# The values' bias of a graph attention moved behind the division, and the values scaled tile by tile

## The chip, the core and the metric

The kernel runs on one core of one Trainium2 chip. A core has a matrix engine (TensorE, PE in the profile), a vector engine (VectorE, DVE), an engine for activation functions (ScalarE, ACT), a general engine (GpSimd, POOL) and an engine that issues transfers (SyncE, SP). [...] The metric is the time of one execution on the device in microseconds (us).

## The reference, cut to what matters

Two layers work on 32 graphs ("batches" below) of 512 nodes with 256 features. Each layer has a graph part and a feed-forward part. The change touches the graph part of the second layer, an attention with 4 heads of 64 features:

```python
h = jnp.einsum('bnd,hde->bhne', nodes_embed, W)
e_src = jnp.einsum('bhne,hte->bhtn', h, a_src)
e_dst = jnp.einsum('bhne,hte->bhtn', h, a_dst)
...
weight = jax.nn.leaky_relu(weight, negative_slope=0.01)
weight = jnp.where(node_adj[:, None] == 0, NEG, weight)
attention = jax.nn.softmax(weight, axis=-1)
dst = jnp.einsum('bhij,bhje->bhie', attention, h) + bias[None, :, None, :]
out = jax.nn.relu(dst) + h
mu = out.mean(axis=-1, keepdims=True)
var = out.var(axis=-1, keepdims=True)
out = (out - mu) / jnp.sqrt(var + EPS) * ln_gamma + ln_beta
```

The weights of a node sum to one. So a bias added to every value `h` before the weighted mean comes out of the mean unchanged; it may be added to the values or to the mean.

## The kernel before, in words

`layer1_plain` computes the second layer. It is written as Python generators that are woven into each other step by step, and a scheduler then orders the instructions of each engine from what was emitted. `attentions` weaves the attention of batch b (`attention(b)`) with the preparation of batch b + 1 (`prepare(b + 1)`) by the counts `TURNS - 4` and `STEPS`; `mixer` runs the feed-forward part for a group of `GB` = 2 batches and pulls the attentions along at a rate `PACE`, in which `STEPS` stands too. So the layer repeats in pairs of batches: the scan of a group (`xp`, `zp`, `yp`, `yTp`, `oTp`, `vp`), then the products `outp` of its two batches, then the slice weights `sw` of the next two, which are softmaxes: `lgp` on TensorE, an exponential on ScalarE (L1336), a product, a sum, a reciprocal and a second product on VectorE (L1337 to L1342), and then the products `yTp` (L1347).

`prepare(b)` gathers the rows of `x` by four indirect DMAs on GpSimd's queue (L1154; five buffers of `x`, so a gather waits for the store of an older batch), normalises them (L1126 to L1133), adds `beta` on GpSimd (L1167), transposes them and computes, for each of NT = 4 tiles of 128 nodes, `hp`: the values of the four heads and the two scores. ScalarE makes four things of each tile (L1183 to L1186): `mine`, the factor exp(s) in the last column of `hv`, `other`, and `ht`, the plain values. Then one instruction on GpSimd adds the bias to all four tiles, from `ht` into `hv` (L1189), and a step of the generator ends. Behind it `mine` is transposed on TensorE (`minep`, L1193), copied by ScalarE, written to DRAM (L1197) and read back spread over all partitions as `own`, by four DMAs on SyncE's queue (L1200). At last VectorE multiplies each tile of the values by its factor (L1202).

`attention(b)` makes the weights on VectorE, one instruction for each head and tile, from `own` and the mask (L1213), and accumulates values and denominators on TensorE (`avp`, `adp`). It takes them back by transposes (`dp`, `bp`), and VectorE divides them into `av`, two heads at a time (L1275). `norm(b, av)` goes on in steps woven into the next batch's attention: the relu and the sum with `ht` (L1290), the mean, the centring, ScalarE's squares, the variance, GpSimd's power (L1300), and the sum into `x` (L1304). GpSimd also adds the output bias to `x` (L1328).

Of the kernel before, what the change touches and what calls it, by code (L numbers as in the profile page):

```python
# [19 lines left out]
P = 128  # L20
N = 512
D = 256
NT = N // P
# [74 lines left out]
def layer0_sorted(tc, ident, eps, x, adj, w, x2s, ranks, over, following):  # L98
# [13 lines left out]
    CAPS = [24, 9, 7, 6, 5, 5, 5] + 5 * [4] + 4 * [3] + 7 * [2] + 9 * [1]  # L112
    STEPS = [16, 12, 9, 8, 7, 6, 5, 4, 3, 2, 1, 0]
    NC = len(STEPS)
    LEAD = 16
# [12 lines left out]
    with ExitStack() as ctx:  # L128
# [22 lines left out]
        steps = cst.tile([P, NC], F32, tag="steps", name="steps")  # L151
        for i, n in enumerate(STEPS):
            nc.gpsimd.memset(steps[:, i : i + 1], n + 0.5)
# [711 lines left out]
def layer1_plain(tc, ident, eps, x2s, ranks, adj, w, out, over, ps):  # L865
# [3 lines left out]
    nc = tc.nc  # L869
# [3 lines left out]
    AH, _, HO = w["W"].shape  # L873
# [13 lines left out]
    HE = HO + 1  # L887
    AP = AH // 2
    TURNS = AP * NT + 6
    STEPS = 15  # L890
    WANTED = 68
    AHEAD = 3
    ATT = 2 * (AHEAD + 2) + AP + 1
# [1 line left out]
    AHEAD_X = 2 * GB + 1  # L895
    PACE = 1.04 * GB * (TURNS + STEPS) / WANTED

# [3 lines left out]
    with ExitStack() as ctx:  # L901
# [6 lines left out]
        def const(name, shape, src):  # L908
            t = ctile(name, shape)
            nc.sync.dma_start(t, src)  # L910
            return t

        def psum(tag, name):
            return ps.tile([P, N], F32, tag=tag, name=name)
# [29 lines left out]
        abias = const("abias", [P, AH * HO], w["gnn_bias"].rearrange("h e -> (h e)").partition_broadcast(P))  # L944
# [203 lines left out]
        def prepare(b):  # L1148

            while b >= AHEAD_X and b - AHEAD_X not in stored:  # L1150
                yield True
            xt = xs[b] = sb.tile([P, NT, D], F32, tag="x", name=f"x{b}", bufs=AHEAD_X)
            for t in range(NT):
                nc.gpsimd.indirect_dma_start(  # L1154
                    out=xt[:, t, :], out_offset=None, in_=x2s[b // SEG],
                    in_offset=bass.IndirectOffsetOnAxis(
                        ap=ranks[:, b * NT + t : b * NT + t + 1].bitcast(U32), axis=0))

            hv = sb.tile([P, NT, AH, HE], F32, tag="hv", name=f"hv{b}")
            xn = hv.rearrange("p t h e -> p (t h e)")[:, : NT * D].rearrange("p (t d) -> p t d", t=NT)  # L1160
            edged = masks(b) if b not in masked else range(3)
            for i, _ in enumerate(edged):
                if i < 3 or b not in masked:
                    yield
                if i == 2:
                    normed(xt, xn, f"c{b}")
                    nc.gpsimd.tensor_add(xt, xt, beta.unsqueeze(1).to_broadcast([P, NT, D]))  # L1167
                    yield
            mask = masked.pop(b)
            xnT = yield from turned(xn, "x3T", f"x3T{b}")  # L1170
            yield


            ht = sb.tile([P, NT, AH * HO], F32, tag="ht", name=f"ht{b}")
            other = sb.tile([P, NT, AH], F32, tag="other", name=f"other{b}")
            mine = sb.tile([P, AH, NT], F32, tag="mine", name=f"mine{b}")
            for t in range(NT):
                ph = psum("any", f"hp{b}_{t}")
                for c in range(DC):
                    nc.tensor.matmul(ph[:, : AH * (HO + 2)], xnT[:, c, t * P : (t + 1) * P], wa[:, c, :],  # L1180
                                     start=c == 0, stop=c == DC - 1)
                d = ph[:, AH * HO : AH * HO + AH]
                nc.scalar.activation(mine[:, :, t], ph[:, AH * (HO + 1) : AH * (HO + 2)], AF.Exp, scale=1.0 - SLOPE)  # L1183
                nc.scalar.activation(hv[:, t, :, HO], d, AF.Exp)
                nc.scalar.activation(other[:, t, :], d, AF.Exp, scale=SLOPE - 1.0)
                nc.scalar.copy(ht[:, t, :], ph[:, : AH * HO])  # L1186
                yield

            nc.gpsimd.tensor_add(hv[:, :, :, :HO], ht.rearrange("p t (h e) -> p t h e", h=AH),  # L1189
                                 abias.rearrange("p (h e) -> p h e", h=AH).unsqueeze(1).to_broadcast([P, NT, AH, HO]))  # L1190
            yield
            pt = psum("any", f"minep{b}")
            nc.tensor.transpose(pt[: AH * NT, :P], mine.rearrange("p h t -> p (h t)"), ident)  # L1193
            row = sb.tile([AH * NT, P], F32, tag="turned", name=f"turned{b}", bufs=1)
            nc.scalar.copy(row, pt[: AH * NT, :P])
            own_row = dr.tile([AH, N], F32, tag="own", name=f"ownd{b}")
            nc.sync.dma_start(own_row.rearrange("h (t p) -> (h t) p", p=P), row)  # L1197
            own = [wide("own", f"own{b}_{h}", AH + 1) for h in range(AH)]
            for h in range(AH):
                nc.sync.dma_start(own[h], own_row[h].partition_broadcast(P))  # L1200
            for t in range(NT):
                nc.vector.tensor_mul(hv[:, t, :, :HO], hv[:, t, :, :HO], hv[:, t, :, HO:].to_broadcast([P, AH, HO]))  # L1202
            ready[b] = mask, ht, hv, other, own
            yield

# [10 lines left out]
        def attention(b):  # L1216

            mask, ht, hv, other, own = ready[b]
            xt = xs[b]
            av = sb.tile([P, NT, AH, HO], F32, tag="av", name=f"av{b}", bufs=1)  # L1220
            turns = [(q, j) for j in range(NT) for q in range(AP)]

            def begin(b, n):
                q, j = turns[n]
                if (b, 2 * q, j) not in weighed:
                    weigh(b, q, j)

            def back(src, kind):

                dst = psum("pv", f"{kind}{b}")  # L1230
                for t in range(NT):
                    nc.tensor.transpose(dst[:, t * P : (t + 1) * P], src[:, t * P : (t + 1) * P], ident)
                return dst

            for n in range(AHEAD):
                begin(b, n)
            pv = [psum("pv", f"avp{b}_{q}") for q in range(AP)]
            for i, (q, j) in enumerate(turns):
                if i + AHEAD < len(turns):
                    begin(b, i + AHEAD)  # L1240
                elif b + 1 in ready:
                    begin(b + 1, i + AHEAD - len(turns))

                if q + 1 == AP:
                    ends = dict(start=j == 0, stop=j == NT - 1)
                    for p in range(AP):
                        for k in range(2 * HO // HW):
                            h, e = 2 * p + k * HW // HO, k * HW % HO
                            nc.tensor.matmul(pv[p][k * HW : (k + 1) * HW, :], hv[:, j, h, e : e + HW],  # L1249
                                             weighed[b, h, j], **ends)  # L1250
                    if j == 0:
                        pd = psum("pv", f"adp{b}")
                    for h in range(AH):
                        nc.tensor.matmul(pd[h * HW : (h + 1) * HW, :], hv[:, j, h, HO:].to_broadcast([P, HW]),
                                         weighed.pop((b, h, j)), **ends)
                yield
                if unfinished and i != 2:
                    next(unfinished[0], None)
                    yield
                    if i > 2:  # L1260
                        unfinished.pop()
            dT = wide("att", f"adT{b}", ATT)
            nc.scalar.copy(dT, pd)
            vT = [wide("att", f"avT{b}_{q}", ATT) for q in range(AP)]
            for q in range(AP):
                nc.scalar.copy(vT[q], pv[q])
            yield
            dt = back(dT, "dp")
            rs = sb.tile([P, NT, AH], F32, tag="rs", name=f"rs{b}")
            nc.vector.tensor_scalar_max(rs, dt.rearrange("p (t h e) -> p t h e", t=NT, h=AH)[:, :, :, 0], 1e-30)  # L1270
            nc.vector.reciprocal(rs, rs)
            for q in range(AP):
                bt = back(vT[q], f"bp{q}_")
                heads = slice(2 * q, 2 * q + 2)
                nc.vector.tensor_mul(av[:, :, heads, :], bt.rearrange("p (t h e) -> p t h e", t=NT, h=2),  # L1275
                                     rs[:, :, heads].unsqueeze(3).to_broadcast([P, NT, 2, HO]))
                yield
            unfinished.append(norm(b, av))

# [28 lines left out]
        def attentions():  # L1308
            yield from prepare(0)
            for b in range(B):  # L1310
                nxt = prepare(b + 1) if b + 1 < B else iter(())
                yield from woven(attention(b), TURNS - 4, nxt, STEPS)
            for _ in unfinished[0]:
# [926 lines left out]
```

## Time and profile before

| what | us |
|---|---|
| median of 3 runs | 4453.05 |
| lowest and highest | 4452.75, 4458.42 |
| the profiled execution's own time | 4459.08 |
| its span | 4456.4 |
| busy: TensorE, VectorE, ScalarE, GpSimd | 3922.0, 3347.2, 2291.6, 1718.8 |

The profile is of one execution. Its span goes from the first instruction to the last, and its own time is 2.7 us longer. Lines such as L1202 are lines of the kernel before; a row of a group gives the engine, the operation, what is written and read, the shape and how often. A row of a tile gives the least, median and largest duration in ns. In the timeline the first two columns are the start and the duration in us, and a bracket at the end of a row tells how long the engine stood idle ahead of it and who ended that.

### The profile page before, as it was taken

The page shows a single profiled execution, that of the slowest core. Times are in us where ns is not written, and L with a number is a line of the kernel's source. Part 1 is how long each engine was busy: PE and PEld are TensorE (multiplying, and loading weights), DVE is VectorE, ACT ScalarE, POOL GpSimd, SP SyncE. Part 2 cuts the span into 40 slices and gives each one's busy share as a digit, 9 for nine tenths or more (in the row PEclk, how much of TensorE's full clock was granted, in tenths as well). Part 3 has the DMA queues.
Part 4 walks back from the last instruction along what each step waited for, and adds up shares of the span by engine and source line. Part 5 has one row for each costly group of instructions (what it writes and reads, how often), then busy time and mean ns, then how long its engine had stood idle before and what let it go on. Part 6 is the DMA issues. An engine that isn't in the chain of part 4 may idle for free.

```text
span 4456.4 us, 57911 instructions
## 1 busy us (share of the span) xinstructions
PE 3922.0 (88%) x20311; PEld 2470.6 (55%) x20311; DVE 3347.2 (75%) x7008; ACT 2291.6 (51%) x4756; POOL 1718.8 (39%) x2036
## 2 busy tenths in 40 slices
PE   5568898899988999888997899999999999999987
PEld 4454565566656656545554455555555555555555
DVE  6668887897788987877766777767677877778763
ACT  3345565566564665556654544544545444454433
POOL 2357644664446644454314232332222232332220
PEclk8679999999999999989998999999999999999998
DMA  5546543664436543564422111111111111111100
GB/s 133 160 144 223 190 130 122 210 200 139 156 117 213 187 147 129 162 201 167 138 81 67 36 53 57 56 48 58 51 43 42 53 55 55 58 48 58 41 15 16
DMA packets 235107, 474.21 MB, mean 106 GB/s; under 512 B 38299, under 2 KB 114075, under 8 KB 234804
## 3 DMA queue, kind: packets, MB, share of 16 engines
q0 software_dynamic: 98688, 315.94, 22.2%
q1 hardware_dynamic: 136116, 154.46, 11.0%
q8 instruction: 162, 2.65, 0.2%
q14 instruction: 141, 1.16, 0.1%
HBM read 413.16 MB, written 57.16 MB: 106 GB/s over the span
## 4 chain that ended last, share of the span: by engine, by line
DVE 34%; PE 32%; DMA 11%; issue 9%; POOL 9%; ACT 5%; SPq 0%; POOLq 0%; DVEq 0%; ACTq 0%
DVE att L1213 5%; DVE acc L637 4%; PE clsp L623 3%; PE avp L1249 3%; PE po L652 3%; PE gatep L623 3%; DMA rows<-table,xs 2%; PE yTp L1347 2%; DVE sw L1337 2%; DVE sw L1342 2%; DVE best L598 2%; DMA rows<-table,tops 2%; DVE sst L1340 2%; DMA best<-table,xs 2%; PE xp L1400 1%
## 5 line engine op out<-in xcount | busy, mean ns | idle before, releaser
L623 PE MATMUL clsp<-xnT,wc 128*128 128x512 f32 x1024 | 520.8, 627 | 49.7 <-ACT cls L625 37.6
L623 PE MATMUL gatep<-xnT,wg 128*128 128x512 f32 x1024 | 499.8, 607 | 10.5 <-ACT gate L625 7.7
L652 PE MATMUL po<-wd,acc 128*128 128x256 f32 x2048 | 455.4, 381 | 6.1 <-DVE acc L641 3.8
L1213 DVE SCALAR_TENSOR_TENSOR att<-own,other,mask 128x512 f32<-128x512 f32 x512 | 392.9, 796 | 79.0 <-DMA own<-ownd 79.0
L652 PEld LDWEIGHTS po<-wd,acc 128*128 128x128 f32 x2048 | 388.3, 191 | 72.1 <-issue 9.2
L598 DVE SCALAR_TENSOR_TENSOR best<-rows,xs,best 128x1024 f32<-128x1024 f32 x212 | 274.4, 1295 | 121.9 <-ACT best L592 76.4
L637 DVE SCALAR_TENSOR_TENSOR acc<-past,fld,acc 128x512 f32<-128x512 f32 x448 | 345.7, 775 | 24.9 <-ACT past L636 16.9
L632 ACT ACTIVATE acc<-tz,fld 128x512 f32<-128x512 f32 x256 | 198.8, 777 | 269.3 <-PE tz L630 240.1
L623 PEld LDWEIGHTS gatep<-xnT,wg 128*128 128x128 f32 x1024 | 196.0, 196 | 252.3 <-issue 197.9
L636 ACT ACTIVATE past<-tz,fld 128x512 f32<-128x512 f32 x448 | 291.4, 693 | 68.1 <-DVE acc L637 66.6
L1347 PE MATMUL yTp<-sw,x 128*128 128x512 f32 x512 | 264.6, 655 | 64.3 <-DVE sw L1342 59.6
L595 POOL DMA_INDIRECT rows<-table,xs x212 | 249.5, 1177 | 171.6 <-DVE best L598 119.0
L1249 PE MATMUL avp<-att,hv 128*32 128x512 f32 x2048 | 298.9, 607 | 5.6 <-DVE att L1213 5.6
L623 PEld LDWEIGHTS clsp<-xnT,wc 128*128 128x128 f32 x1024 | 181.5, 198 | 188.1 <-issue 111.8
L434 PE MATMUL pm<-h,adj 128*128 128x258 f32 (+1 forms) x1024 | 181.2, 324 | 99.9 <-DVE keep L427 33.7
L1300 POOL TENSOR_TENSOR mu<-mu,eps 128x16 f32<-128x16 f32 x32 | 111.6, 3487 | 391.1 <-DVE mu L1299 391.0
L1335 PE MATMUL lgp<-wsl,x4T 128*128 128x512 f32 x512 | 242.8, 613 | 15.7 <-ACT sw L1336 6.8
L1154 POOL DMA_INDIRECT x<-x2s,ranks x128 | 135.9, 1062 | 298.1 <-DVE att L1213 148.1
L625 ACT ACTIVATE gate<-gatep,fld 128x512 f32<-128x512 f32 x256 | 175.5, 685 | 142.6 <-PE gatep L623 123.8
L553 POOL DMA_INDIRECT xs<-rows_of,order x128 | 156.1, 1219 | 221.5 <-DVE acc L637 100.8
L1567 PE MATMUL outp<-v,swT 128*128 128x256 f32 x1024 | 227.6, 381 | 0.0
L625 ACT ACTIVATE cls<-clsp,fld 128x512 f32<-128x512 f32 x256 | 176.1, 688 | 93.9 <-PE clsp L623 55.6
(599 smaller groups left out, 8978.1 us busy)
## 6 DMA issues: line engine op xcount, KB each, us to landing
adj<-in_adj POOLq DMA_DIRECT2D x128, 256.0 KB
ai<-in_adj SPq DMA_DIRECT2D x128, 256.0 KB
own<-ownd SPq DMA_DIRECT2D x128, 256.0 KB
rows_of<-keep SPq DMA_DIRECT2D x32, 550.0 KB
x<-in_x SPq DMA_DIRECT2D x32, 512.0 KB
x2s<-xs SPq DMA_DIRECT2D x32, 512.0 KB
out<-x SPq DMA_DIRECT2D x32, 512.0 KB
rows<-table,xs POOLq DMA_INDIRECT x212
```

The costliest lines, as they stand in the source:

```text
L595: nc.gpsimd.indirect_dma_start(out=row, out_offset=None, in_=table, in_offset=bass.IndirectOffsetOnAxis(ap=idxs[:, k : k + 1].bitcast(U32) ...
L598: nc.vector.scalar_tensor_tensor(m, row, vals[:, k : k + 1], m, ALU.add, ALU.max)
L623: nc.tensor.matmul(pf, wf[:, c, f * P : (f + 1) * P], xnT[:, c, :], start=c == 0, stop=c == DC - 1)
L625: nc.scalar.activation(o, pf, fn, bias=fld[:, f, bf : bf + 1], scale=1.0 if fn == AF.Gelu else 0.5)
L636: nc.scalar.activation(r, z, AF.Relu, bias=fld[:, f, AT + b : AT + b + 1])
L637: nc.vector.scalar_tensor_tensor(y, r, fld[:, f, CH + b : CH + b + 1], y, ALU.mult, ALU.add)
L652: nc.tensor.matmul(po[:, i, :], acc[f][:, t * P : (t + 1) * P], wd[:, f, :], start=f == 0, stop=f == FC - 1)
L1213: nc.vector.scalar_tensor_tensor(e, own[h], other[:, j, h : h + 1], mask[:, j, :], ALU.max, ALU.mult)
L1249: nc.tensor.matmul(pv[p][k * HW : (k + 1) * HW, :], hv[:, j, h, e : e + HW], weighed[b, h, j], **ends)
L1335: nc.tensor.matmul(pf, xnT[:, c, t * P : (t + 1) * P], wsl[:, c, :], start=c == 0, stop=c == DC - 1)
L1347: nc.tensor.matmul(py, xn[:, t, c * P : (c + 1) * P], sw[:, t, :], start=t == 0, stop=t == NT - 1)
L1567: nc.tensor.matmul(po[:, :D], swT[:, k, t * P : (t + 1) * P], v[:, k, :], start=k == 0, stop=k == KC - 1)
```

## The change

The bias is no longer added to the values. The division's result `av` gets it instead, for two heads at a time, by GpSimd. The values are scaled from `ht` straight into `hv`, by VectorE: tile t - 1 right after ScalarE's four instructions on tile t, and the last tile after the loop. The step that ended behind the old addition is gone, so `STEPS` is 14 instead of 15.

```diff
-    STEPS = 15
+    STEPS = 14
...
+            def values(t):
+                nc.vector.tensor_mul(hv[:, t, :, :HO], ht[:, t, :].rearrange("p (h e) -> p h e", h=AH),
+                                     hv[:, t, :, HO:].to_broadcast([P, AH, HO]))
+
             for t in range(NT):
...
                 nc.scalar.copy(ht[:, t, :], ph[:, : AH * HO])
+                if t:
+                    values(t - 1)
                 yield
 
-            nc.gpsimd.tensor_add(hv[:, :, :, :HO], ht.rearrange("p t (h e) -> p t h e", h=AH),
-                                 abias.rearrange("p (h e) -> p h e", h=AH).unsqueeze(1).to_broadcast([P, NT, AH, HO]))
-            yield
+            values(NT - 1)
             pt = psum("any", f"minep{b}")
...
-            for t in range(NT):
-                nc.vector.tensor_mul(hv[:, t, :, :HO], hv[:, t, :, :HO], hv[:, t, :, HO:].to_broadcast([P, AH, HO]))
             ready[b] = mask, ht, hv, other, own
...
                 nc.vector.tensor_mul(av[:, :, heads, :], bt.rearrange("p (t h e) -> p t h e", t=NT, h=2),
                                      rs[:, :, heads].unsqueeze(3).to_broadcast([P, NT, 2, HO]))
+
+                nc.gpsimd.tensor_add(av[:, :, heads, :], av[:, :, heads, :],
+                                     abias.rearrange("p (h e) -> p h e", h=AH)[:, heads, :].unsqueeze(1)
+                                     .to_broadcast([P, NT, 2, HO]))
                 yield
```

## The prediction, made before the changed kernel was run

> **What bounds the kernel now.** The change touches the second layer alone, from 2400 us to the end. I read the page first (the whole span, and the chain that ended last), then the table by stages for the steady part of that layer, then the groups of TensorE there, then the two tiles that the change handles, and last the timeline of one pair of batches.
>
> ```profile
> span 4456.4 us, 57911 instructions
> PE 3922.0 (88%) x20311; PEld 2470.6 (55%) x20311; DVE 3347.2 (75%) x7008; ACT 2291.6 (51%) x4756; POOL 1718.8 (39%) x2036
> ...
> DVE 34%; PE 32%; DMA 11%; issue 9%; POOL 9%; ACT 5%; SPq 0%; POOLq 0%; DVEq 0%; ACTq 0%
> ```
>
> ```profile
> sum 1600.00, PE 1486.21 PEld 887.36 DVE 1183.05 ACT 790.15 POOL 468.84; mean PE 185.78 PEld 110.92 DVE 147.88 ACT 98.77 POOL 58.61
> ```
>
> The second fence is the sum row of the stages from 2600 to 4200 us. TensorE (PE) is busy 1486.2 of 1600 us, 92.9%. So at most 7.1% of this part can be won without giving TensorE less work. The layer goes in pairs of batches; in the chain of waits the first products of the scan (`xp`) start at 3036.44 and at 3162.74, so a pair takes 126 us and TensorE is idle for some 8.9 us of it. Who holds it up stands in the groups of the stretch 2600 to 4250:
>
> ```profile
> L1347 PE MATMUL yTp<-sw,x 128*128 128x512 f32 x432 | 227.5, 665 | 61.3 <-DVE sw L1342 56.8 <-DVE sst L1341 2.7 <-ACT ai L1094 0.6
> L1335 PE MATMUL lgp<-wsl,x4T 128*128 128x512 f32 x428 | 201.5, 607 | 11.2 <-ACT sw L1336 6.8 <-DVE x L1569 2.9 <-DVE mask L1085 1.1
> L1535 PE MATMUL oTp<-yT,hoT 128*128 128x128 f32 x416 | 49.9, 278 | 12.4 <-ACT yT L1529 12.4
> ```
>
> The largest part, 59.5 us, is the product of the slice weights waiting for VectorE (DVE) to finish their softmax. So VectorE sets the end only where it is late with `sw`. Adding the idle stretches in the timeline of PE over eleven pairs gives 3.9 us a pair in the half of the even batch, 2.9 us in that of the odd one (1.9 before `yTp`, 1.0 before `rnp`), and 1.0 before `oTp`.
>
> VectorE's own two long waits here (tiles `hv` and `att`, the first with its row for GpSimd):
>
> ```profile
> L1202 DVE TENSOR_TENSOR hv<-hv x128: 415/419/427, 2409.2 to 4260.7; 128x256 f32<-128x256 f32 x128
> L1189 POOL TENSOR_TENSOR hv<-ht,abias x32: 2327/2355/7253, 2404.6 to 4256.7; 128x1024 f32<-128x1024 f32 x32
> ...
>   POOL hv L1189: 177.5, 31
> ...
>   DMA own<-ownd: 79.0, 15
> ```
>
> 177.5 us in 31 waits is 5.7 us a batch, but only some of that reaches TensorE: most falls where TensorE has other work queued.
>
> [...] (VectorE and GpSimd rows of the timeline):
>
> ```profile
> 2890.28 2.92 POOL L1167 TENSOR_TENSOR x<-x,beta 128x1024 f32<-128x1024 f32 x1 [10.31 <-ACT hv L1133]
> 2891.00 2.75 DVE L1213 SCALAR_TENSOR_TENSOR att<-own,other,mask 128x512 f32<-128x512 f32 x1
> ...
> 2411.74 10.68 DVE L1213 SCALAR_TENSOR_TENSOR att<-own,other,mask 128x512 f32<-128x512 f32 x16
> 2417.41 7.25 POOL L1189 TENSOR_TENSOR hv<-ht,abias 128x1024 f32<-128x1024 f32 x1 [10.47 <-ACT ht L1186]
> ```
>
> A weight of 0.74 us took 2.75 beside an addition; an addition of 2.35 took 7.25 behind a row of sixteen weights. The old addition nearly always ran while VectorE stood waiting for it, so it cost no lock; the new ones run among the weights. [...] here 2.355 us against 1.217 for 128x1024. No row has GpSimd's addition of 128x512. Bounds: half of 2.355 is 1.18, and no size makes it dearer than 2.36. I take 1.25 us each.
>
> **Part 1, the old addition goes (32 of 2.355 us), and the scaling follows each tile.** In the odd batch of the pair at 3200 us, VectorE waits from 3250.9 to 3259.80 and scales until 3261.8, one piece of it inside the softmax. ScalarE's last copy of `ht` ends at 3257.34. With the new code three tiles are scaled before that and the fourth ends at about 3257.9. The next work, the softmax of `sw`, needs ScalarE's exponential, which ends at 3259.09; it started at 3260.82. So 1.6 us earlier, and 0.34 us of scaling has left the chain: 2.0 us. Against 1.9 us of TensorE's idle time before `yTp` I take 1.3 us, since not each pair has it in this place. In the even batch (wait 3317.2 to 3321.36) nothing is won by this: VectorE then waits for `msp` until 3323.66 and for `own` until 3328.74.
>
> **Part 2, one step less in the preparation moves the transpose of `mine`.** The instruction order of the two built programs shows it: in the even batches from 2 to 30 `minep` stands ahead of `oTp` and `msp` in 1 of 15 before and in 12 of 15 after, so it moves in 11. In the pair at 3300 us the last exponential of `mine` ends at 3318.51, but `minep` ran at 3323.54, and the chain ownd, own, att followed until 3328.74. Placed right after `yTp` (ends 3318.33), its copy waits for ScalarE's copy of `yT` (ends 3319.39) and is done near 3319.6 instead of 3324.10. The two DMAs keep their 4.6 us, and SyncE's queue is clear (the last `ai` load ahead was issued at 3316.24): `att` starts at 3324.2, 4.5 us earlier. By 11/15 that is 3.3 us of lead for VectorE. TensorE has its `vp` and `outp` products until some 3342, so nothing shows at once; it shows where `sw` is late afterwards. The order also puts `bp1` of the odd batch ahead of the second `outp` group in 12 of 14 pairs (4 before), so that its division comes before those sums.
>
> **Part 3, the new additions: 64 of 1.25 us.** Each waits for its division on VectorE (L1275, 0.68 us[...]), and the norm's first instruction (L1290) waits for both. Even batches: divisions end at 0 and 0.6; the first addition runs 0.2 to 1.45, beside the second division. Then come five weights (3.3 us) and the norm; the first weight stands until 1.45 (0.85 lost). The second addition either wins the lock (1.25 lost) or starves until the weights end and the norm waits 1.4: 2.1 us lost either way. Odd batches: the order leaves one sum and one weight (1.0 us) between division and norm, and the norm comes at 3.4 instead of 1.6: 1.8 us lost. At least 0.9 us (the adds find gaps), at most 2.6 us (both in full). Behind the additions in GpSimd's queue stand `mu`'s power and, in odd batches, the eight gathers of `x`; those waited for the store of an older `x` anyway (start 3338.98), and I cost them at nothing as long as `bp1` comes first.
>
> **The sum per pair.** Odd half: `yTp` gains 1.3; the lead of 2.0 us is eaten by the lock (2.1) before `rnp`, whose 1.0 stays. Even half: lead 3.3 - 1.8 = 1.5 us off the 3.9. `oTp`: `minep` fills 0.3 of its 1.0. Total 3.1 us, over 15 pairs 47 us. The profiled execution took 4459.1 us (the span and 2.7 around it), 6.0 more than the median of 4453.05; 4459.1 - 47 - 6 gives 4406.
>
> **Rivals.**
> 1. *The lock cancels the gain.* With 2.6 us lost in each half, leads of 2.0 and 3.3 leave nothing in the odd half and 0.7 us in the even; new waits of `minep`'s neighbours eat that. For it: VectorE's atts are in rows, as at 2411.74. Against: VectorE is busy only 74% here (1183 of 1600). Time 4453.
> 2. *Slower: the gathers queue behind the additions.* Where `bp1` still comes after the second `outp` (3342.35 in this trace), the division ends near 3344 and the additions near 3346.7, so the gathers start 7.7 us late; VectorE's statistics of the next `x` (L1126) wait for them in order, with the softmax behind. The leads of 1.5 and the gains of 1.6 elsewhere cover 3.1 us of delay; from there it decides. For it: L1126 already waits 43.0 us on these DMAs. Against: the order of `bp1`. At 5 us a pair, 1.9 x 15 = 28 us: 4481.
> 3. *More than forecast.* If VectorE is never late with `sw`, 6 of 8.9 us go: 90 us, 4363. For it: the chain holds GpSimd's addition and both `own` DMAs in every pair. Against: the lock, and TensorE's clock at 0.97 to 0.99 already.
>
> **How the numbers follow.** Chances: forecast 0.57, rival 1 0.15, rival 2 0.21, rival 3 0.07. The forecast alone spans 4385 to 4432, from the bounds of the lock (0.9 to 2.6 us) and of what TensorE gets of each lead. With the other cases the range is 4375 to 4475. What the measurement can tell from no change is 0.2%, 9 us: faster is under 4444. That gives 0.64 faster (forecast, rival 3, a little of rival 1), 0.13 the same, 0.23 slower.
>
> **What would show it.** Right: VectorE's wait on `hv` falls from 177.5 us to below 90 and ends at ScalarE's copy; the wait for `own` (79.0) falls by half or more; `yTp`'s wait for `sw` (56.8 in the stretch) falls to about 30; TensorE's share rises from 92.9% to about 95%; single atts of about 2 us stand beside the new additions. Wrong: L1126's wait for the gathers grows well over 43 us, or the norm's first instruction waits over 2 us a batch for GpSimd.

## The result and the profile after

| | before | after |
|---|---|---|
| median, us | 4452.9 (4 runs, 4450.26 to 4458.42) | 4553.83 (4 runs, 4550.85 to 4562.9) |
| ratio after to before | | 1.0228, 95% interval 1.0211 to 1.0246 |
| profiled execution: span, own time | 4456.4, 4459.08 | 4552.2, 4553.97 |
| mean period of a pair of batches, us | 123.5 | 129.9 |

The change makes the kernel 2.3% slower, 101 us, where 47 us of gain were forecast. The period is the mean distance between the first scan products `xp` of two groups, over 14 pairs; 14 times 6.4 us is 90 us, so nearly all of the loss is in the steady part of the second layer.

From the page of the kernel after: the span, the busy times, and the shares of the chain that ended last.

```profile
span 4552.2 us, 57959 instructions
...
PE 3950.6 (87%) x20311; PEld 2480.8 (54%) x20311; DVE 3432.5 (75%) x7008; ACT 2291.2 (50%) x4756; POOL 1737.8 (38%) x2068
...
PE 37%; DVE 31%; DMA 9%; POOL 9%; issue 8%; ACT 5%; SPq 0%; POOLq 0%; DVEq 0%; ACTq 0%
```

VectorE (DVE) is busy 85 us longer with the same 7008 instructions. The table by stages of the kernel after, 2600 to 4200 us as in the prediction: its last stage and the sum. A stage's row has its length, the busy time and number of instructions of PE, PEld, DVE, ACT and POOL, the granted TensorE clock, the DMA share and GB/s.

```profile
4000.00:4200.00 200.00, 174.36 (x1083) 107.64 (x1082) 139.41 (x268) 89.12 (x236) 63.67 (x46) 0.91 0.19 57
sum 1600.00, PE 1431.04 PEld 849.30 DVE 1186.73 ACT 743.51 POOL 470.60; mean PE 178.88 PEld 106.16 DVE 148.34 ACT 92.94 POOL 58.83
```

TensorE (PE) was busy 92.9% of this stretch and is now 89.4%. Of a pair that is 8.8 us of idle time before (7.1% of 123.5) and 13.7 after (10.6% of 129.9): 4.9 of the 6.4 us are gaps. The other 1.5 us are longer work, and the clock fits that: the granted clock averages 0.958 over the eight stages, 0.978 before, and is down to 0.91 in the last. The clock record of both traces holds two rates only, full and half, and a pair has 11.5 us at half rate, 5.9 before. In these pairs each stretch at half rate comes behind 3.413 us in which TensorE was idle for 45% of the time or more (the last section has the numbers). So more gaps came here with a lower clock, and a pair grew by more than its gaps.

Which gaps? The groups of TensorE in the stretch 2600 to 4250, after:

```profile
L1354 PE MATMUL yTp<-sw,x 128*128 128x512 f32 x416 | 211.6, 650 | 64.8 <-DVE sw L1349 56.2 <-DVE mask L1085 8.0
L1342 PE MATMUL lgp<-wsl,x4T 128*128 128x512 f32 x406 | 205.9, 643 | 20.6 <-ACT sw L1343 8.1 <-DVE stc L1126 4.5 <-DVE mask L1085 3.4
...
L1542 PE MATMUL oTp<-yT,hoT 128*128 128x128 f32 x384 | 46.1, 278 | 8.0 <-ACT yT L1536 7.4 <-ACT turned L1200 0.6
...
L1084 PE MATMUL maskp<-identb,a 128*128 128x128 bf16 x396 | 38.7, 230 | 38.5 <-DVE mask L1085 32.7 <-ACT sw L1343 4.3 <-DVE x L1576 1.6
```

The wait for `sw` before `yTp` is what it was (56.2 us after 56.8), in 26 batches instead of 27. New is a product that the prediction does not name: `maskp`, which transposes the adjacency, waits 32.7 us for VectorE's cast of an earlier mask (3.3 before). The waits of the same stretch (engine and line, what it waited for, us in total, times, longest), first of the kernel before:

```profile
DVE att L1213 <- DMA own<-ownd: 72.8, 13, 7.3
...
DVE stc L1126 <- DMA x<-x2s,ranks: 31.6, 35, 1.7
...
DVE av L1303 <- POOL mu L1300: 19.8, 13, 2.1
...
PE maskp L1084 <- DVE mask L1085: 3.3, 4, 1.0
```

and of the kernel after:

```profile
DVE hv L1179 <- ACT ht L1191: 83.3, 55, 3.1
...
DVE av L1310 <- POOL mu L1307: 70.5, 22, 6.4
...
DVE stc L1126 <- DMA x<-x2s,ranks: 32.7, 22, 3.5
...
DVE att L1216 <- DMA own<-ownd: 28.9, 20, 5.4
...
DVE av L1297 <- POOL av L1281: 12.5, 12, 1.2
```

VectorE's waits moved much as forecast. The wait on `hv` now ends at ScalarE's copy, though over the whole run it fell only from 177.5 to 104.9 us and not below 90. The wait for `own` has fallen by more than half, the gathers cost no more in total, and the norm's first instruction (L1297) hardly waits for the additions. TensorE's two signs failed: neither did `yTp` wait less, nor did its busy share rise. The wait that grew is the second of the kernel after: the norm's last product (L1303 before, L1310 now) waits for GpSimd's power of the variance, 70.5 us against 19.8, at most 6.4 us at a time against 2.1. One such place in the timeline of the kernel after, first VectorE, then GpSimd, then TensorE:

```profile
2995.19 0.17 DVE L1306 TENSOR_SCALAR mu<-mu 128x16 f32<-128x16 f32 x1
2995.27 0.75 DVE L1216 SCALAR_TENSOR_TENSOR att<-own,other,mask 128x512 f32<-128x512 f32 x1
3000.54 1.23 DVE L1310 TENSOR_TENSOR av<-av,mu 128x1024 f32<-128x1024 f32 x1 [4.52 <-POOL mu L1307]
3001.68 0.68 DVE L1085 CAST mask<-maskp 128x512 uint8<-128x512 bf16 x1
...
3003.41 3.84 DVE L1344 TENSOR_TENSOR sw<-sw,ebsl 128x512 f32<-128x512 f32 x2
...
2995.27 1.02 POOL L1154 DMA_INDIRECT x<-x2s,ranks  x1 [0.19 <-issue]
2996.60 0.95 POOL L1154 DMA_INDIRECT x<-x2s,ranks  x1 [0.30 <-issue]
2997.57 2.93 POOL L1307 TENSOR_TENSOR mu<-mu,eps 128x16 f32<-128x16 f32 x1
...
3002.41 0.59 PE L1084 MATMUL maskp<-identb,a 128*128 128x128 bf16 x4 [8.98 <-DVE mask L1085]
```

The variance is ready at 2995.36. GpSimd has two gathers to issue first, and its power of only 16 numbers in each partition takes 2.93 us. VectorE stands 4.52 us, and the mask's cast and the softmax of `sw`, which come behind the product in its order, start at 3001.68 and 3003.41; TensorE, which needs the cast, stands 8.98 us. In the kernel before the softmax stood ahead of that product in each of these odd batches, and gave the power time. The softmax of batch b - 1 has eight products on VectorE, four with `ebsl` (L1337) and four with `sst` (L1342). How many of them stand ahead of the norm's last product of the odd batch b in VectorE's order, for b = 3 to 29:

```text
before, e2, e4               8 in 14 of 14
after, e1, e3, e8, e9        8 in 3, 0 in 11 of 14
e6, e10                      0 in 14 of 14
e11                          0 or 1 in 9, 7 or 8 in 5 of 14
e5, e7, e13, e15             8 in 14 of 14
e12, e14                     7 or 8 in 14 of 14
```

### The profile page after: what moved, and what is told of

The parts are those of the page before. It is cut to its first block, busy times and chain, and to the rows that moved or that the text cites. A ratio compares the mean times of both kernels' runs of the same rounds, so it can differ in the third digit from the quotient of the medians.

```text
span 4552.2 us, 57959 instructions
## 1 busy us (share of the span) xinstructions
PE 3950.6 (87%) x20311; PEld 2480.8 (54%) x20311; DVE 3432.5 (75%) x7008; ACT 2291.2 (50%) x4756; POOL 1737.8 (38%) x2068
## 4 chain that ended last, share of the span: by engine, by line
PE 37%; DVE 31%; DMA 9%; POOL 9%; issue 8%; ACT 5%; SPq 0%; POOLq 0%; DVEq 0%; ACTq 0%
DVE att L1216 5%; PE avp L1252 4%; DVE acc L637 4%; PE clsp L623 3%; PE gatep L623 3%; PE po L652 3%; PE yTp L1354 2%; DMA rows<-table,xs 2%; DVE best L598 2%; DVE sw L1344 2%; PE hp L1185 2%; PE adp L1257 2%; POOL x L1154 2%; PE lgp L1342 2%; DMA rows<-table,tops 2%
## 5 line engine op out<-in xcount | busy, mean ns | idle before, releaser
L623 PE MATMUL clsp<-xnT,wc 128*128 128x512 f32 x1024 | 521.6, 628 | 56.8 <-ACT cls L625 43.9
L1216 DVE SCALAR_TENSOR_TENSOR att<-own,other,mask 128x512 f32<-128x512 f32 x512 | 405.4, 821 | 32.5 <-DMA own<-ownd 32.3
L1354 PE MATMUL yTp<-sw,x 128*128 128x512 f32 x512 | 256.3, 643 | 67.7 <-DVE sw L1349 56.2
L1252 PE MATMUL avp<-att,hv 128*32 128x512 f32 x2048 | 308.8, 613 | 6.3 <-DVE att L1216 6.1
L1342 PE MATMUL lgp<-wsl,x4T 128*128 128x512 f32 x512 | 258.6, 643 | 25.2 <-ACT sw L1343 9.7
L434 PEld LDWEIGHTS pm<-h,adj 128*128 128x128 f32 x1024 | 149.7, 210 | 127.9 <-issue 71.0
L1574 PEld LDWEIGHTS outp<-v,swT 128*128 128x128 f32 x1024 | 192.2, 190 | 30.3 <-ACT v L1566 5.4
```

The source lines that it names most:

```text
L434: nc.tensor.matmul(pm[:, : c1 - c0], a[:, i, t * P : (t + 1) * P], h[:, i, c0:c1], start=i + c0 == 0, stop=i + 1 == NT and c0 > 0)
L623: nc.tensor.matmul(pf, wf[:, c, f * P : (f + 1) * P], xnT[:, c, :], start=c == 0, stop=c == DC - 1)
L1216: nc.vector.scalar_tensor_tensor(e, own[h], other[:, j, h : h + 1], mask[:, j, :], ALU.max, ALU.mult)
L1342: nc.tensor.matmul(pf, xnT[:, c, t * P : (t + 1) * P], wsl[:, c, :], start=c == 0, stop=c == DC - 1)
L1354: nc.tensor.matmul(py, xn[:, t, c * P : (c + 1) * P], sw[:, t, :], start=t == 0, stop=t == NT - 1)
L1574: nc.tensor.matmul(po[:, :D], swT[:, k, t * P : (t + 1) * P], v[:, k, :], start=k == 0, stop=k == KC - 1)
```

## The experiments

The runs came in four groups; the kernel before, run along with them, had medians of 4459.2, 4465.39, 4459.17 and 4460.44 us. So kernels are compared by their ratios to it.

| run | what | median | ratio, 95% interval |
|---|---|---|---|
| e1 | after, no additions | 4492.71 | 1.0080, 1.0060 to 1.0101 |
| e2 | before, bias moved only | 4474.38 | 1.0034, 1.0025 to 1.0043 |
| e3 | before, step dropped only | 4520.04 | 1.0151, 1.0126 to 1.0177 |
| e4 | after, step put back | 4481.78 | 1.0059, 1.0038 to 1.0080 |
| e5 | after, pace 1.00 | 4525.0 | 1.0129, 1.0112 to 1.0146 |
| e6 | before, pace 1.06 | 4514.63 | 1.0101, 1.0080 to 1.0121 |
| e7 | e3, pace 1.00 | 4517.1 | 1.0115, 1.0094 to 1.0137 |
| e8 | e3, product doesn't wait for the power | 4455.71 | 0.9978, 0.9965 to 0.9990 |
| e9 | after, product doesn't wait for the power | 4484.67 | 1.0054, 1.0037 to 1.0070 |
| e10 | e3, product two turns later | 4571.34 | 1.0253, 1.0236 to 1.0270 |
| e11 | after, additions on VectorE | 4464.74 | 1.0012, 1.0003 to 1.0022 |
| e12 | e3, power on VectorE | 4443.93 | 0.9964, 0.9952 to 0.9977 |
| e13 | after, power on VectorE | 4480.09 | 1.0045, 1.0033 to 1.0056 |
| e14 | e13, additions on VectorE too | 4430.91 | 0.9932, 0.9906 to 0.9958 |
| e15 | before, power on VectorE | 4474.45 | 1.0029, 1.0019 to 1.0038 |

### The change taken apart: e1 to e4

"Lock" stands in the prediction, in the expectations and below for what the traces show: an instruction of VectorE or GpSimd that takes longer beside one of the other engine. In the kernel after, 54 of 512 weights took 0.80 us or more, 1.39 in their median, and 52 of these ran beside an addition of GpSimd; the others took 0.74 in their median, among them 47 beside GpSimd's power.

e1 is the changed kernel without its additions; the bias is left out.

```diff
-                nc.gpsimd.tensor_add(av[:, :, heads, :], av[:, :, heads, :],
-                                     abias...)
```

> The changed kernel with the new additions on GpSimd taken out: the bias is not added at all, the rest is as changed. Theory G (the 64 additions cost the time, through VectorE's lock and GpSimd's queue): 4400 to 4455 us, ratio to before 0.99 to 1.00. Theory S (the dropped step, which reorders TensorE, VectorE and GpSimd, costs the time): stays near 4530 to 4550, ratio 1.017 to 1.022.

e2 is the kernel before with the additions moved, the scaling where it was, and the step kept.

```diff
-            nc.gpsimd.tensor_add(hv[:, :, :, :HO], ht..., abias...)
             yield
...
-                nc.vector.tensor_mul(hv[:, t, :, :HO], hv[:, t, :, :HO], hv[:, t, :, HO:]...)
+                nc.vector.tensor_mul(hv[:, t, :, :HO], ht[:, t, :]..., hv[:, t, :, HO:]...)
...
+                nc.gpsimd.tensor_add(av[:, :, heads, :], av[:, :, heads, :], abias...)
```

> Only the bias moves: added behind the division by GpSimd, the values scaled from ht in the old place after the loop, the old step kept (STEPS 15). Theory G: 4530 to 4560 (ratio 1.02). Theory S: 4440 to 4460 (ratio 0.998 to 1.002), since the order of minep and bp1 is that of before.

e3 is the kernel before with nothing but the step dropped.

```diff
-    STEPS = 15
+    STEPS = 14
...
             nc.gpsimd.tensor_add(hv[:, :, :, :HO], ht..., abias...)
-            yield
```

> Only the step goes: the kernel before with the step behind GpSimd's addition dropped and STEPS 14; the old addition and the old scaling stay. Theory G: 4410 to 4455 (ratio 0.99 to 1.0), as own comes earlier. Theory S: 4530 to 4560 (ratio 1.02).

e4 is the changed kernel with the step put back.

```diff
-    STEPS = 14
+    STEPS = 15
...
             values(NT - 1)
+            yield
```

> The changed kernel with the step put back (a yield behind the last scaling, STEPS 15): new additions and tile-by-tile scaling stay. Theory G: 4530 to 4560 (ratio 1.02). Theory S: 4430 to 4460 (ratio 0.995 to 1.002).

None of the four lies in a range that was given. e2, e3 and e4 lie nearer to theory S, the dropped step; e1 lies between the two theories. The step alone costs 1.5%, more than everything else together in the old order (e4, 0.6%). It moves no work to another engine and adds none, so what costs is the order. e1 and e2 only seem at odds: leaving out the additions takes 1.5% off the changed kernel (e1), while moving the bias in the old order costs 0.3% (e2). But e2 also drops the old addition, and with it VectorE's wait for it (145.9 us before in this stretch; 51.6 in e2, for ScalarE's copy). The waits of e3, same stretch:

```profile
DVE av L1302 <- POOL mu L1299: 63.9, 23, 5.1
...
PE yTp L1346 <- DVE sst L1340: 22.8, 5, 7.2
...
PE lgp L1334 <- DVE mask L1085: 20.7, 8, 4.7
```

The wait for the power is there without any new addition (19.8 before), and TensorE's new waits are for what stands behind it: the softmax's reciprocal (2.7 before) and the mask (1.1 before).

### The order by itself: e5 to e7

How the steps of the attentions fall against the mixer is set by `PACE`, in which `STEPS` stands. A small move of its factor turns the order in the built programs without any other edit, so it can stand in for the step.

```diff
-    PACE = 1.04 * GB * (TURNS + STEPS) / WANTED
+    PACE = 1.00 * GB * (TURNS + STEPS) / WANTED
```

for e5 (on the kernel after) and e7 (on e3), and 1.06 for e6 (on the kernel before).

> The changed kernel with the planner's pace lowered from 1.04 to 1.00 and nothing else. In the built program this puts all eight last products of the softmax of sw ahead of the norm's last product again in all 14 pairs, and minep behind oTp, as before the change, though the step stays dropped. Theory O (it is the order that costs): time near that of the run with the step put back (4482), 4465 to 4490, VectorE's wait for the power of the norm back to about 20 us in the stretch 2600 to 4250. Rival (the dropped step or GpSimd's additions cost by themselves, whatever the order): 4530 to 4560.

> The kernel before with the planner's pace raised from 1.04 to 1.06 and nothing else: no instruction is added or removed, but the order turns to the new one (the norm's last product ahead of the softmax of sw in all 14 pairs, minep ahead of oTp in 15 of 15). Theory O: slower, 4505 to 4550, with VectorE's wait for the power above 60 us in the stretch. Rival (the order costs nothing by itself): 4445 to 4465.

> The kernel before with the step dropped alone, as in e3_step_only (4520), but the pace at 1.00, so that the order is the old one. Theory O: the loss of e3_step_only goes, 4440 to 4475. Rival (the missing step itself costs, for instance by issuing the preparation's DMAs at other times): 4500 to 4530.

e6 came out as theory O has it: with no instruction added or removed, the turned order costs 1.0%, and VectorE waits for the power (though the pace moves other work too). From its waits:

```profile
DVE av L1303 <- POOL mu L1300: 79.4, 26, 5.1
```

e5 and e7 did not. The softmax is ahead again and the wait for the power is 23.0 us in both, yet both kernels stay slow. In e5 and e7 another wait stands in its place, from the waits of e5:

```profile
PE maskp L1084 <- ACT sw L1343: 58.1, 13, 4.8
```

It was 7.0 us before, and is 29.7 in e7. A pace of 1.00 shifts all of the attention's steps against the mixer, not only the one in question. So the order matters, but these two runs say nothing of the power: that the softmax stands ahead is not enough for a fast order. e7 even lies in its rival's range, the missing step itself; only e8 below sets that aside.

In e7 most of the loss is not a wait. Its TensorE is even fuller than before (1496.0 of 1600 us), with the products of the weights and the values, `avp`; first the kernel before, then e7:

```profile
L1249 PE MATMUL avp<-att,hv 128*32 128x512 f32 x1680 | 240.4, 607 | 0.0
...
L1248 PE MATMUL avp<-att,hv 128*32 128x512 f32 x1664 | 281.6, 601 | 0.0
```

A single product is as long as before (601 ns after 607), but together they keep TensorE busy 41 us longer in this stretch. So fewer of them run beside each other: by these rows 4.2 in the mean before (1680 x 607 ns in 240.4 us) and 3.6 in e7 (1664 x 601 in 281.6). In TensorE's order they stand in 286 unbroken rows instead of 198, and only 39 rows have all sixteen products of a tile, 65 before. e5 has the same (284.1 us, 279 rows, 39 full). The order at this pace thus has a cost of its own, which the traces show and no run tested by itself.

### The wait by itself: e8, e9 and e10

e8 (on e3) and e9 (on the kernel after) keep their order and all instructions, and take away what the product waits for: the power goes to a tile that nobody reads, and the product multiplies by the variance itself. So both leave the power out of the layer's result.

```diff
+            pw = sb.tile([P, NG], F32, tag="pw", name=f"pw{b}")
...
-            nc.gpsimd.tensor_tensor(mu[:, 1, :], mu[:, 1, :], eps..., ALU.pow)
+            nc.gpsimd.tensor_tensor(pw, mu[:, 1, :], eps..., ALU.pow)
```

> The same order as e3_step_only (4520: the step dropped alone), but GpSimd's power goes to a tile of its own and the norm's last product multiplies by the variance itself, so that VectorE does not wait for GpSimd there (the power is left out of the layer's result; every instruction is still issued). Theory O in its narrow form (what costs in the new order is VectorE standing before GpSimd's power with the softmax and the masks queued behind): 4445 to 4480. Rival (it is the place of the norm's work and of minep in the order, not this wait): 4505 to 4525.

> The changed kernel in its own order, but with the norm's last product multiplying by the variance itself, while GpSimd's power goes to a tile of its own (the power is left out of the layer's result, every instruction is issued). Theory W (the loss is mostly VectorE standing before GpSimd's power): the 1.7% that this took off e3_step_only come off here too, 4470 to 4490, and the rest, 15 to 25 us, is the additions' lock. Rival L (in the changed kernel the additions' lock with VectorE and their place in GpSimd's queue cost some 60 us by themselves): 4510 to 4540.

Both came out as the theory of the wait has it. By the ratios, the wait is worth 1.7% in e3 (0.9978 over 1.0151) and 1.7% in the changed kernel (1.0054 over 1.0228), some 75 us. In e9 `maskp` waits 13.5 us for the mask instead of 32.7. Without the wait the dropped step is no loss but a small gain (0.2%), and the rest of the change costs 0.8% (1.0054 over 0.9978). Two groups of VectorE in this stretch have grown, e8 first:

```profile
L1212 DVE SCALAR_TENSOR_TENSOR att<-own,other,mask 128x512 f32<-128x512 f32 x420 | 322.8, 799 | 31.5 <-DMA own<-ownd 31.3
...
L1201 DVE TENSOR_TENSOR hv<-hv 128x256 f32<-128x256 f32 x104 | 38.1, 420 | 167.8 <-POOL hv L1189 167.8
```

and e9:

```profile
L1216 DVE SCALAR_TENSOR_TENSOR att<-own,other,mask 128x512 f32<-128x512 f32 x416 | 331.6, 825 | 30.8 <-DMA own<-ownd 30.3
...
L1179 DVE TENSOR_TENSOR hv<-ht,hv 128x256 f32<-128x256 f32 x104 | 63.1, 631 | 83.6 <-ACT ht L1191 83.6
```

In the same order a weight takes 825 ns in the mean instead of 799, and a tile's scaling 631 instead of 420. The second was not in the forecast at all: once it no longer waits for GpSimd's old addition, the scaling runs beside GpSimd's other work. In the trace of the kernel after, 15 of the 128 scalings took 0.97 to 2.29 us, 2.25 in their median, each beside GpSimd's addition of the output bias, and the other 113 took 0.42. Over the whole run VectorE is busy 70 us longer in e9 than in e8 (3422.9 after 3352.6).

e10 tried to cure e3 by calling the last product later, with nothing left out.

```diff
-                if unfinished and i != 2:
+                if unfinished and i not in (2, 3, 4):
...
-                    if i > 2:
+                    if i > 4:
```

> The kernel before with the step dropped (as e3_step_only, 4520), and the norm's last product and sum called two turns of the weights later, with nothing left out. Theory W: VectorE has weights to do in those turns, the wait for the power falls from 64 us in the stretch to below 15, and the time to 4440 to 4475. Rival (what the product's wait held back, the masks and sst, is held back as much by the product's later place, or the later sum delays the slices): 4500 to 4525.

It is the slowest of all. The wait for the power did fall to 11.6 us, but the order changed elsewhere too (`minep` ahead of `oTp` in 15 of 15 batches instead of 12), and other work came too late; from the waits of e10:

```profile
DVE rn L1353 <- ACT swT L1352: 91.4, 13, 9.0
...
PE maskp L1084 <- DVE mask L1085: 27.8, 6, 6.6
...
PE yTp L1526 <- DVE y L1521: 26.4, 9, 5.9
```

The rival was right here in its kind, and the time lies above its range too: taking a wait away by moving the waiter moves what hangs on it.

### The additions off GpSimd: e11

```diff
-                nc.gpsimd.tensor_add(av[:, :, heads, :], av[:, :, heads, :],
+                nc.vector.tensor_add(av[:, :, heads, :], av[:, :, heads, :],
```

> The changed kernel with the 64 new additions on VectorE in place of GpSimd: no lock and nothing of theirs in GpSimd's queue, but some 64 x 0.61 = 39 us of VectorE's own time. Theory L (lock and queue of the additions on GpSimd cost about 60 us in this order): near the run without the additions (4493) plus what of the 39 us reaches the end, 4495 to 4525. Theory W (the place of the additions matters little): 4540 to 4570.

It is faster than either theory had it, but it is no clean measure of the lock: with more work on VectorE the order turned halfway back (the table above), and the wait for the power fell to 27.1 us.

### The power off GpSimd, nothing left out: e12 to e15

The power of the variance is worked out on VectorE: a first value from a shift and a subtraction on the bits, then two Newton steps.

```diff
-            nc.gpsimd.tensor_tensor(mu[:, 1, :], mu[:, 1, :], eps..., ALU.pow)
+            yv = sb.tile([P, 2, NG], F32, tag="yv", name=f"yv{b}")
+            vr, y0, y1 = mu[:, 1, :], yv[:, 0, :], yv[:, 1, :]
+            nc.vector.tensor_scalar(y0.bitcast(I32), vr.bitcast(I32), 1, None, ALU.logical_shift_right)
+            nc.vector.tensor_scalar(y0.bitcast(I32), y0.bitcast(I32), -1.0, float(0x5F3759DF), ALU.mult, ALU.add)
+            for _ in range(2):
+                nc.vector.tensor_mul(y1, y0, y0)
+                nc.vector.scalar_tensor_tensor(y1, y1, -0.5, vr, ALU.mult, ALU.mult)
+                nc.vector.scalar_tensor_tensor(y0, y1, 1.5, y0, ALU.add, ALU.mult)
...
-            nc.vector.tensor_mul(heads, heads, mu[:, 1, :]...)
+            nc.vector.tensor_mul(heads, heads, y0...)
```

e12 does this to e3, e13 to the kernel after, e15 to the kernel before; e14 is e13 with the edit of e11.

> The kernel before with the step dropped (e3_step_only, 4520), and the power of the norm worked out on VectorE by eight small operations of 128x16 (a shift and a subtraction for a first value, two Newton steps) in place of GpSimd's 3.3 us: VectorE no longer waits for GpSimd there. Theory W: the loss goes, and at most some 1 us a batch is paid for the eight operations: 4425 to 4465. Rival (the order with the step dropped costs by something else as well): 4490 to 4525.

> The changed kernel with the same power on VectorE and the additions still on GpSimd. Theory W: as e9_after_no_wait, 4465 to 4495. Rival (the additions need the old order, their lock decides): 4515 to 4555.

> As e13, with the additions on VectorE too. If the additions' lock makes the 29 us between e8 and e9, this is 10 to 25 us faster than e13 although VectorE has 39 us more of its own. If the moved scaling makes them, it is as slow as e13 or slower by up to 30 us.

> The kernel before, step and order kept, with the power on VectorE alone. In the old order VectorE waits only 20 us for the power in the stretch, so theory W gives little: 4435 to 4465, that is 0 to 20 us better. Rival (GpSimd's 3.3 us of the power holds up something else too, the gathers behind it): below 4430.

e12 and e13 confirm e8 and e9 with nothing left out: the loss goes in both. (In these the scheduler also puts the softmax ahead again; e8 and e9, where it does not, are about as fast, so it is the wait and not the place.) e15 is the control: in the old order, where the wait is short, the same edit doesn't help but costs 0.3%, which lies above the range given. So the power is no burden by itself, only where VectorE stands before it. e14 then answers the second question. The weights and the scaling in e13:

```profile
L1216 DVE SCALAR_TENSOR_TENSOR att<-own,other,mask 128x512 f32<-128x512 f32 x417 | 332.6, 821 | 31.3 <-DMA own<-ownd 30.7
...
L1179 DVE TENSOR_TENSOR hv<-ht,hv 128x256 f32<-128x256 f32 x104 | 68.4, 676 | 64.2 <-ACT ht L1191 63.8
```

and in e14, with the additions in their new place:

```profile
L1216 DVE SCALAR_TENSOR_TENSOR att<-own,other,mask 128x512 f32<-128x512 f32 x428 | 312.7, 754 | 28.0 <-DMA own<-ownd 27.3
...
L1179 DVE TENSOR_TENSOR hv<-ht,hv 128x256 f32<-128x256 f32 x108 | 59.5, 572 | 46.5 <-ACT ht L1191 45.2
...
L1281 DVE TENSOR_TENSOR av<-av,abias 128x512 f32<-128x512 f32 x54 | 34.9, 681 | 0.0
```

Taking the additions off GpSimd is worth 1.1% (0.9932 over 1.0045), about twice what was expected of the lock. A weight falls from 821 to 754 ns, and over the whole run VectorE is busy no longer (3445.6 us after 3449.5) though it does 45.2 us of additions more: its other instructions had been longer by about as much in e13. (An addition took 681 ns; the 0.61 us of the expectations was an estimate, half of VectorE's 1.22 us for 128x1024.) Lock and GpSimd's queue were not told apart further. e14 beats both kernels, 0.7% faster than before; the sum of its stages from 2600 to 4200:

```profile
sum 1600.00, PE 1500.54 PEld 900.71 DVE 1285.68 ACT 798.27 POOL 319.52; mean PE 187.57 PEld 112.59 DVE 160.71 ACT 99.78 POOL 39.94
```

TensorE is busy 93.8% of it (92.9% before), VectorE 80% (74%) and GpSimd 20% (29%). A pair takes 121.4 us.

## Why the prediction was wrong

**What bounds the kernel** was read rightly: VectorE's lateness is what TensorE waits for. But the prediction looked at the waits that were long before, and the loss came in one that was short: 19.8 us of VectorE for the power. Its two signs of being wrong looked elsewhere as well, and neither showed.

**Part 1 was right in its mechanism.** The old addition's wait went, and the scaling starts once ScalarE's copy is there. The forecast was 1.3 us a pair, 20 us in all. e1 against e3 measures it without the new additions, in the order after and with the same wait for the power (63.3 and 63.9 us): 0.7% (1.0080 over 1.0151), some 31 us. With power and additions on VectorE, the moved bias and scaling gain 0.3% (0.9932 over 0.9964), 14 us. Only in the old order, with the additions on GpSimd, is scaling tile by tile no faster than scaling late (e4, 1.0059; e2, 1.0034). What it left out is that the scaling lost its cover from the lock: 572 to 676 ns a tile in the groups above instead of 420.

**Part 2 is the step that failed.** "One step less in the preparation moves the transpose of `mine`" priced the dropped step by `minep`, `own` and `bp1` alone, as a gain of lead, since these were the instructions looked for in the new order. They moved as said, and the wait for `own` fell. But the same step moved the norm's last product ahead of the softmax in 11 of 14 odd batches. This wait costs 1.7% (e8 against e3, e9 against the kernel after), some 75 of the 101 us. It does not turn the sign alone: without it the kernel after is still 0.5% slower than before (e9). Without the wait the step gains between 0.2% (e8) and 0.6% (e12 over e15: 0.9964 over 1.0029), 10 to 29 us. The forecast's terms for it, ahead of the additions' lock that e8 and e12 don't have, were (3.3 + 0.3) x 15 = 54, two to five times as much.

**Part 3 had the additions' cost about right, but not what covers it.** The lock was priced at 2.1 and 1.8 us a batch, 3.9 us a pair; the kernel after over e1 gives 1.5%, some 65 us, 4.4 us a pair. (An addition took 1.49 us in the median of the stretch, 1.26 at least, instead of the 1.25 estimated from GpSimd's 2.355 us for 128x1024, where VectorE's operations took 1.217. The divisions, priced without a lock, had none in the kernel after: all 64 took 0.67 to 0.69 us, though 26 ran for over half of that beside an addition of GpSimd.) Leads of 2.0 and 3.3 us were to cover it. The runs give a loss of 0.8% for the additions and the moved scaling together, 34 us or 2.3 us a pair (e9 over e8), and 1.1% for having the additions on GpSimd rather than on VectorE (e14 against e13). And "Behind the additions in GpSimd's queue stand `mu`'s power and ... I cost them at nothing" named the very instruction, but did not ask who waits for the power.

**The parts as measured.** The step alone -0.2% (e8), its wait for the power 1.7% (e3 over e8), the old addition's end and the scaling -0.7% (e1 over e3) and the new additions 1.5% (the kernel after over e1) make the 2.3%. e9, which is not in this chain, finds the same 1.7% for the wait.

**The rivals.** Rival 2 had the right side and the right kind of mechanism, GpSimd's queue with VectorE standing in order before it, but the wrong place: L1126 waited no more for the gathers (32.7 us after 31.6). At 4481 it was also far too small, since it had no part for the masks and for the lost clock (0.958 after 0.978). Rival 1, the lock cancels the gain, is near to what e4 and e9 show, where the long wait for the power is absent, though these are slower by 0.5% to 0.6% and not level.

**Still open:** whether the broken rows of `avp` are all that makes the pace of 1.00 slow (e5, e7), and how much of e14's gain over e13 is the lock and how much GpSimd's shorter queue.

## What to carry to other kernels

Where a change drops or moves a step of a woven schedule, compare the order of all instructions on each engine, not only of those that the change handles, and for each pair that changed places ask what the one now ahead waits for and what stands behind it. A wait that is short because other work happens to lie in front of it is a debt: work out what it costs when that work goes. To find out if a wait is to blame, take away what it waits for and keep the order (e8, e9); moving the waiter (e10) or the whole schedule (e5, e7) brings other costs in and settles nothing.

## What the runs showed of the hardware

- GpSimd's power of 128x16 took 3.34 us in the median of the kernel before, nearly three times VectorE's product of 128x1024 (1.22 us), and more than GpSimd's own addition of 128x1024 (2.355 us). The eight small operations of 128x16 on VectorE that stand in for it in e14 took 0.16 to 0.17 us each in the median, some 1.3 us together, where at most some 1 us had been estimated.
- Over the 14 pairs of the period TensorE's clock record has 17 stretches at half rate before and 27 after, all of them 3.413 us long or two to four times that. In the 3.413 us ahead of such a stretch TensorE was idle for 45 to 87% of the time before and for 52 to 100% after; ahead of 3 of the 27 the profile has no product at all. In the stretch from 2600 to 4200 us as a whole it was idle for 7.1% before and 10.6% after. That the idle time brings the half rate was not tested by itself.
- The lock shows in the kernel after in a new place. Of the norm's 32 last products (1.22 us in the median) 7 took 3.37 us in their median, each beside GpSimd's addition of `beta`. In the timeline below the addition of 2.33 us had begun 0.06 us ahead of the product, and the product ended 1.10 us behind it:

```profile
3658.37 3.37 DVE L1310 TENSOR_TENSOR av<-av,mu 128x1024 f32<-128x1024 f32 x1 [6.43 <-POOL mu L1307]
...
3658.31 2.33 POOL L1167 TENSOR_TENSOR x<-x,beta 128x1024 f32<-128x1024 f32 x1
```
